# Linear attention and feed-forward on one core: another beginning, a query tile ahead, and weights cast later

## The chip, the cores and the metric

The kernel runs on one core of one Trainium2 chip. The metric is the device time of one execution in microseconds. The times shown are medians of several executions. A profiled execution is one of its own; its times are what the profile and the trace show.

## What is computed

The input `x` is 16 sequences of 1024 rows of 512 numbers. Cut to what matters, the reference is:

```python
qkv = x @ Wqkv.T + bqkv
q, k, v = split(qkv)
q, k = rope(rmsnorm(q, gq)), rope(rmsnorm(k, gk))     # 16 heads of 32
qf, kf = relu(q), relu(k)
vk = einsum('bhlp,bhld->bhpd', [v, 1], kf)             # summed over a sequence
res = einsum('bhpd,bhld->bhlp', vk, qf)
attn = res[..., :-1] / (res[..., -1:] + 1e-6)
x = layernorm(x + rmsnorm(attn @ Wout.T + bout, gout))
xr, xk = mu_r*x + (1-mu_r)*x_prev, mu_k*x + (1-mu_k)*x_prev
r = sigmoid(xr @ W_r.T);  k_act = relu(xk @ W_k.T)**2
x = layernorm(x + r * (k_act @ W_v.T))
```

## The kernel before

The rows are worked in 128 tiles of 128 rows; 8 tiles make a sequence. Every operand of a large product is held as two fp32r parts: a high part, cast by ACT (`S.copy`), and the rest, which DVE or POOL makes by subtraction. A product is then three matmuls (high by high, high by low, low by high).

The first half of the run goes through the tiles in *slots*. Slot `i`:

- loads the transposed tile `i + 2` (`load_xt`) and the plain tile `i + 1` (`load_xn`), and splits them (`split_x`, `split_xn`);
- projects tile `i` onto queries and keys (`proj(i, 0)` and `proj(i, 1)`, 12 matmuls each, L426). The bias is put into the bank ahead by a copy on ACT (`seed`, through the helper at L157); for the first two tiles it is added by two further matmuls from a row (L436);
- turns both by the rope tables (`rope`): ACT sums squares (L453), DVE multiplies twice and adds (L456 to L458), POOL takes the power (L142), ACT scales and clips the keys (L468, L469), DVE makes their low part (L470), POOL adds up the keys of the sequence (L475, L477);
- takes the rope tables of tile `i + 1` (`tables`). For the first 8 tiles they are made: one matmul (L388) and a copy by ACT (L389), one product by POOL (L385), and stores to memory (L390). Later tiles load them (L380);
- multiplies the keys of tile `i - 1` with its rows (`add_kx`, 12 matmuls, L496), summed in four banks over the sequence.

At the end of a sequence `finish_a` empties the four banks (L510 by ACT, L511 by DVE), `finish_s` sums the keys, `finish_b` and `finish_c` make the matrix that the sequence's queries are multiplied with, and `finish_c` stores it (L589, 512 KB each). They stand in slots with `i % 8` equal to 1 to 6. The 20 weight pieces that are needed later are loaded one a slot from slot 5 on (`late_weight`, the load at L352, the cast at L353, the low part at L354); 12 of them are stored again, split (L605). From slot 26 on the matrices of the first sequence are loaded (`load_m`), and from slot 30 on the first tiles of the second half are begun (`FIRST`, `STEP`).

Four banks of PSUM (`bank`) go round for projections, tables and seeds; four more (`kx_bank`) hold the key sums, and serve the beginning before that.

Ahead of slot 0 stands the beginning: ten matmuls on zeros (`NWARM`), loads of the query and key weights in eight pieces (`stage_qk`, L631, the first four turn about on the queues of SP and ACT), their split (`split_qk`, L638, L639), the bias and gain rows (L645), the masks and tables (`gt`, L705 to L707, and `cs`, L717 to L728), and the projections of tiles 0 and 1.

Order: `in_order` fixes the traced order on an engine. In the beginning it holds for all engines, for slots 0 to 7 on PE alone. Elsewhere a planner orders the instructions by its own estimate of time. `tc.issue_after` keeps loads behind a given one on SP.

The second half multiplies the queries with the matrices and does the feed-forward part (L178). Nothing there is touched.

Of the kernel before, what the change touches and what calls it, by code (L numbers as in the profile page):

```python
# [15 lines left out]
P = 128  # L16
# [8 lines left out]
NWARM = 10  # L25
# [8 lines left out]
def kernel(  # L34
# [58 lines left out]

    @contextmanager
    def in_order(engine):

        traced = nc.cur_bb.bb.instructions
        n = len(traced)
        yield
        assert traced is nc.cur_bb.bb.instructions  # L100
        last = None
        for i in traced[n:]:
            if i.engine != engine:
                continue
            if last is not None:
                tc.add_manual_dep(
                    i,
                    last.name,
                    mybir.DependencyInfo(
                        mybir.DependencyClass.NoSync, mybir.DependencyReason.DATA  # L110
                    ),
                    reason="in_order",
                )
            last = i
# [190 lines left out]
    with ExitStack() as a_ctx:  # L305
# [44 lines left out]
        def split_w(hi, lo, src, low, dma, tag="xw", bufs=3):  # L350
            w = tp.tile([P, DIM], F32, tag=tag, bufs=bufs, name="wstage")
            dma.dma_start(out=w, in_=src)  # L352
            S.copy(hi, w)  # L353
            low.tensor_sub(lo, w, f32(hi))  # L354

        first = {}

        def seed(i):
            for j in range(2):
                first[i, j] = seeded(f"ps{'qk'[j]}{i}", b_qk[:, j * DIM : (j + 1) * DIM])  # L360
# [7 lines left out]
        tab, tab_d = {}, {}  # L368

        def tables(i):  # L370

            t = i % 8
            if i < 8:
                tab_d[t] = dram.tile([P, 2, 2, DIM], F32, name=f"tab_d{t}")
            for j in range(2):
                for n in (1, 0):
                    tb = wa.tile([P, DIM], F32, tag=f"tab{j}{n}", name=f"tab{j}{n}{i}")
                    tab[i, j, n] = tb
                    if i >= 8:
                        nc.sync.dma_start(out=tb, in_=tab_d[t][:, j, n, :])  # L380
                        continue
                    g = g_qk[:, j * DIM : (j + 1) * DIM]
                    if n == 0:
                        c = angle[0][:, t, :].unsqueeze(1).to_broadcast([P, 2 * HEADS, HH])
                        G.tensor_mul(rows(tb), rows(g), c)  # L385
                    else:
                        ps = kx_bank(j) if i < 2 else bank(f"pstab{i}{j}")
                        T.matmul(ps, lhsT=cs[0:KT, t, :], rhs=gt[0:KT, j, :], start=True, stop=True)  # L388
                        S.copy(tb, ps)  # L389
                    nc.sync.dma_start(out=tab_d[t][:, j, n, :], in_=tb)  # L390
# [3 lines left out]
        def constants():  # L394
            nc.sync.dma_start(out=b_out, in_=bout.partition_broadcast(P))
            nc.sync.dma_start(out=g_out, in_=gout.partition_broadcast(P))
            for n, m in (("k", mu_k), ("r", mu_r)):
                mu[n] = const.tile([P, NC_], F32, name=f"mu_{n}")
                nc.sync.dma_start(out=mu[n], in_=m)
                omm[n] = const.tile([P, NC_], F32, name=f"omm_{n}")  # L400
                V.tensor_scalar(omm[n], mu[n], -1.0, 1.0, ALU.mult, ALU.add)
# [7 lines left out]

        mask = te.tile([P, P], BF16, name="mask")  # L410
        V.memset(mask, 0.0)
        for h in range(P // DH):
            V.memset(mask[h * DH : (h + 1) * DH, h * DH : (h + 1) * DH], 1.0)
        ones = te.tile([P, P], F32R, name="ones")
        V.memset(f32(ones), 1.0)
# [3 lines left out]
        def proj(i, j):  # L419

            seeds = i > 1
            ps = first.pop((i, j)) if seeds else bank(f"ps{'qk'[j]}{i}")
            cols = slice(j * DIM, (j + 1) * DIM)
            for c in range(NC_):
                for n, (a, b) in enumerate(((xh, "h"), (xh, "l"), (xl, "h"))):
                    T.matmul(  # L426
                        ps,
                        lhsT=a[i][:, c, :],
                        rhs=w_qk[b][:, c, cols],
                        start=(not seeds and c == 0 and n == 0),  # L430
                        stop=(seeds and c == NC_ - 1 and n == 2),
                        skip_group_check=True,
                    )
# [12 lines left out]
        acc, ros = {}, {}  # L446

        def rope(i, ps):

            ss = wa.tile([P, 2], F32, tag="ss", bufs=3, name=f"ss{i}")  # L450
            ro = []
            for j in range(2):
                S.activation(junk(f"{i}{j}"), ps[j], AF.Square, accum_out=ss[:, j : j + 1])  # L453
                r = wa.tile([P, DIM], F32, tag=f"ro{j}", bufs=1 + j, name=f"ro{j}{i}")
                t2 = wa.tile([P, DIM], F32, tag="t2", name=f"t2{j}{i}")
                V.tensor_mul(t2, ps[j], tab.pop((i, j, 1)))  # L456
                V.tensor_mul(ps[j], ps[j], tab.pop((i, j, 0)))
                V.tensor_add(halves(r), halves(ps[j]), halves(t2)[:, :, ::-1, :])  # L458
                ro.append(r)
                if j == 0:  # L460
                    q_d[i] = dram.tile([P, DIM], F32, name=f"q_d{i}")
                    nc.sync.dma_start(out=q_d[i], in_=r)
            V.tensor_scalar(ss, ss, 1.0 / DIM, RMS_EPS, ALU.mult, ALU.add)  # L463
            rsqrt(rstd_all[:, i, :], ss)
            k = ro[1]
            kh = tk.tile([P, DIM], F32R, tag="kh", bufs=2, name=f"kh{i}")
            kl = tk.tile([P, DIM], F32R, tag="kl", bufs=2, name=f"kl{i}")
            S.activation(kh, k, AF.Relu, scale=rstd_all[:, i, 1:2])  # L468
            S.activation(k, k, AF.Relu, scale=rstd_all[:, i, 1:2])  # L469
            V.tensor_sub(kl, k, f32(kh))  # L470
            b, t = divmod(i, 8)
            ros[i] = k
            if t == 1:
                acc[b] = tx.tile([P, DIM], F32, tag="acc", name=f"acc{b}")
                G.tensor_add(acc[b], ros[i - 1], k)  # L475
            if t > 1:
                G.tensor_add(acc[b], acc[b], k)  # L477
            return kh, kl
# [118 lines left out]
        def late_weight():  # L597
            n, w, c = late.pop(0)
            if n in "ao":
                to = {"a": w_a, "o": w_o}[n]  # L600
                split_w(to["h"][:, c, :], to["l"][:, c, :], w[:, c, :], V, nc.sync)
                return
            m = te.tile([P, 2, DIM], F32R, tag="m", bufs=2, name=f"w{n}{c}")
            split_w(m[:, 0, :], m[:, 1, :], w[:, c, :], V, nc.sync)
            nc.sync.dma_start(out=w_d[n][:, c, :, :], in_=f32(m))  # L605
# [7 lines left out]
        start_pe.enter_context(in_order(mybir.EngineType.PE))  # L613
        start = a_ctx.enter_context(ExitStack())
        for e in ("SP", "Activation", "DVE", "Pool"):
            start.enter_context(in_order(getattr(mybir.EngineType, e)))

        row = tp.tile([P, DIM], F32, tag="q", bufs=3, name="row")
        V.memset(row, 0.0)
        m0 = te.tile([P, 2, DIM], F32R, tag="m", bufs=2, name="m0")  # L620
        V.memset(f32(m0[:, 0, :]), 0.0)


        for n in range(NWARM):
            T.matmul(bank(f"pswarm{n}"), lhsT=m0[:, 0, 0:P], rhs=m0[:, 0, :], start=True, stop=True)
        stage = {}

        def stage_qk(j, c, dma=nc.sync):
            n = NC_ * j + c
            w = tp.tile([P, DIM], F32, name="wstage", **[dict(tag="x", bufs=NT), dict(tag="xw", bufs=3), dict(tag="q", bufs=3)][(n >= NT) + (n >= NT + 3)])  # L630
# [3 lines left out]
        def split_qk(j, c, low=V):  # L634
# [4 lines left out]
            low.tensor_sub(l, w, f32(h))  # L639
# [4 lines left out]
        for n, src in enumerate((bqkv[0 : 2 * DIM], gqk)):  # L644
            nc.scalar.dma_start(  # L645
# [3 lines left out]

        S.copy(table, mhalf)  # L650
        angle = [tp.tile([P, 8, HH], F32, tag="y", bufs=2, name=f"angle{n}") for n in range(2)]
        nc.sync.dma_start(out=angle[1], in_=sin_t)
        stage_qk(1, 0)
        load_xt(1)
        for c in range(1, NC_):
            stage_qk(1, c)
        load_xn(0)
        nc.sync.dma_start(out=angle[0], in_=cos_t)
        g_qk = wp.tile([P, 2 * DIM], F32, tag="m", bufs=NC_, name="g_qk")
        nc.sync.dma_start(out=g_qk, in_=gqk.partition_broadcast(P))  # L660
        b_qk = ca.tile([P, 2 * DIM], F32, name="b_qk")
# [20 lines left out]
        V.tensor_scalar(msk[:, 1, :], msk[:, 0, :], -1.0, None, ALU.mult)  # L682
        cs6 = wp.tile([P, 8, P], F32, tag="m", bufs=NC_, name="cs6")[:, :, 0:KT]
# [5 lines left out]
        split_qk(0, 0)  # L689
        split_qk(0, 1)  # L690
# [4 lines left out]
        split_qk(0, 2)  # L695
        split_qk(0, 3)
        ahead = {(0, 0): proj(0, 0)}
        split_x(1)
        split_qk(1, 0, G)
        split_qk(1, 1, G)  # L700
        gt = wp.tile([P, 2, DIM], F32R, tag="m", bufs=NC_, name="gt")
        for j in range(2):
# [8 lines left out]
            )  # L711
        cs = wp.tile([P, 8, P], F32R, tag="m", bufs=NC_, name="cs")
# [16 lines left out]
        split_qk(1, 2, G)  # L729
        split_qk(1, 3, G)  # L730
        ahead[1, 0] = proj(1, 0)
        tables(0)
        ahead[0, 1] = proj(0, 1)
        split_xn(0)
        ahead[1, 1] = proj(1, 1)
        start.close()

        def slot(i):
# [6 lines left out]
            qk = [ahead.pop((i, j)) if i < 2 else proj(i, j) for j in range(2)]  # L745
            if 0 < i < N - 1:
                split_x(i + 1)
            if i > 0:
                split_xn(i)
# [8 lines left out]
            if i >= 1:  # L758
                add_kx(i - 1)
            state[i] = rope(i, qk)  # L760
            if not last:
                tables(i + 1)
                if i > 0:
                    seed(i + 1)
            if i == 2:
                with tc.issue_after(load.ins):
                    constants()
            if i >= 5 and late:
                with tc.issue_after(load.ins):
                    late_weight()  # L770
            j, late_by = divmod(i - FIRST, STEP)
            if j + 1 in (0, NPRE) and late_by >= STEP - NC_:

# [321 lines left out]
```

## Time and profile before

| | us |
|---|---|
| median of the runs shown | 2727.32 (2726.01 to 2727.47) |
| the profiled execution | 2726.91 |
| its span | 2725.1 |
| PE busy in it | 2694.3 |
| DVE, ACT, POOL busy | 2168.5, 1882.8, 706.5 |
| mean granted TensorE clock | 0.997 |
| first matmul, first projection | 2.23, 7.58 |

The engines work side by side, each through its own queue in order: PE the matmuls, DVE and ACT element-wise work, POOL slow element-wise work, SP the transfers (`SPq` is its issuing, `ACTq` that of ACT). A row of the timeline gives the start, the duration, engine, line and operation, then what is written and read; the brackets give how long the engine had been idle and what ended that. The share of busy time is a mean over all stages, so it is read by stretches of time.

### The profile page before, as it was taken

The numbers are of one execution on the slowest core, as the hardware profiler recorded it, in microseconds if no ns is written. First come the engines' busy times: TensorE is split into PE (matmuls) and PEld (weight loads), VectorE is DVE, ScalarE is ACT, GpSimd is POOL, SyncE is SP. The second block draws the span as 40 slices with busy tenths as digits, with TensorE's granted clock in tenths as the row PEclk, the third lists the DMA queues.
The fourth block names the chain that finished last, engine by engine and source line by source line (L and its number), as shares of the span: only waits on it lengthen the run. The fifth ranks groups of instructions, "written<-read, shape, count | busy, mean of one in ns | idle before, by whom it ended". The sixth has DMA issues, their size and how long they took to land.

```text
span 2725.1 us, 40195 instructions
## 1 busy us (share of the span) xinstructions
PE 2694.3 (99%) x12558; PEld 2231.9 (82%) x12558; DVE 2168.5 (80%) x4876; ACT 1882.8 (69%) x3822; POOL 706.5 (26%) x804
## 2 busy tenths in 40 slices
PE   8999999999999999999999999999999999999998
PEld 6788788888888888887888888888888888888887
DVE  7878787877787787776888878888887878888874
ACT  6666565666666666657777787777777777777775
POOL 5222222222222222224322222222222222222221
PEclk9999999999999999999999999999999999999999
DMA  7689777777777877764332232323133232313210
GB/s 237 210 301 320 228 247 229 229 224 226 232 229 254 265 248 243 230 204 159 105 94 86 93 109 66 109 89 113 62 97 109 72 99 93 116 59 106 77 54 36
DMA packets 232014, 433.28 MB, mean 159 GB/s; under 512 B 24676, under 2 KB 24932, under 8 KB 231800
## 3 DMA queue, kind: packets, MB, share of 16 engines
q1 hardware_dynamic: 231504, 430.18, 49.0%
q8 instruction: 99, 1.62, 0.2%
q14 instruction: 115, 0.94, 0.1%
q10 hardware_dynamic: 296, 0.53, 0.1%
HBM read 314.19 MB, written 116.42 MB: 158 GB/s over the span
## 4 chain that ended last, share of the span: by engine, by line
PE 51%; DVE 1%; ACT 0%; issue 0%; POOL 0%; POOLq 0%; ACTq 0%
PE psk L178 12%; PE psv L178 12%; PE psr L178 12%; PE psy L178 11%; PE pst L163 2%; PE psqt L163 2%; ACT x L283 0%; DVE mixr L832 0%; DVE q L235 0%; DVE mixk L832 0%; DVE gate L973 0%; DVE mrl L848 0%; DVE qtl L247 0%; ACT gate L961 0%; DVE den L232 0%
## 5 line engine op out<-in xcount | busy, mean ns | idle before, releaser
L178 PE MATMUL psk<-mkh,w_k 128*128 128x512 f32 x1024 | 332.7, 396 | 1.1 <-DVE kx L511 0.7
L178 PE MATMUL psv<-w_v,kah 128*128 128x512 f32 x1024 | 321.6, 395 | 1.3 <-DVE gate L973 1.0
L178 PE MATMUL psy<-mb,qth 128*128 128x512 f32 x1024 | 319.9, 389 | 0.3 <-ACT qth L246 0.3
L178 PE MATMUL psr<-w_r,mrh 128*128 128x512 f32 x1024 | 318.6, 396 | 0.0
L477 POOL TENSOR_TENSOR acc<-acc,ro 128x512 f32<-128x512 f32 x96 | 159.0, 1656 | 270.4 <-ACT ro L469 227.4
L178 PEld LDWEIGHTS psy<-mb,qth 128*128 128x128 f32 x1024 | 192.0, 188 | 40.4 <-ACT qth L246 0.7
L178 PEld LDWEIGHTS psk<-mkh,w_k 128*128 128x128 f32 x1024 | 191.3, 188 | 40.3 <-DVE kx L511 1.0
L178 PEld LDWEIGHTS psv<-w_v,kah 128*128 128x128 f32 x1024 | 187.7, 188 | 38.6 <-DVE gate L973 1.5
L178 PEld LDWEIGHTS psr<-w_r,mrh 128*128 128x128 f32 x1024 | 188.7, 188 | 36.9 <-ACT r L883 0.2
L142 POOL TENSOR_TENSOR rstd_all<-ss,mhalf 128x2 f32<-128x2 f32 x128 | 93.8, 733 | 477.6 <-DVE ss L463 459.7
L848 POOL TENSOR_TENSOR mkl<-mixk,mkh 128x512 fp32r<-128x512 f32 x127 | 166.0, 1307 | 181.7 <-ACT mkh L846 177.3
L426 PE MATMUL psq<-wqk_h,xh 128*128 128x512 f32 x512 | 201.7, 394 | 4.0 <-ACT psq L157 3.2
L426 PE MATMUL psk<-wqk_h,xh 128*128 128x512 f32 x512 | 199.8, 390 | 2.5 <-ACT psk L157 2.5
L426 PE MATMUL psq<-wqk_l,xh 128*128 128x512 f32 x512 | 200.5, 392 | 0.9 <-DVE wqk_l L639 0.8
L426 PE MATMUL psq<-wqk_h,xl 128*128 128x512 f32 x512 | 200.6, 392 | 0.0
L178 PE MATMUL psv<-w_v,kal 128*128 128x512 f32 x512 | 200.1, 391 | 0.0
L178 PE MATMUL psk<-mkl,w_k 128*128 128x512 f32 x512 | 199.8, 391 | 0.2 <-DVE mkl L848 0.2
L178 PE MATMUL psy<-mb,qtl 128*128 128x512 f32 x512 | 199.6, 390 | 0.0
L426 PE MATMUL psk<-wqk_h,xl 128*128 128x512 f32 x512 | 199.3, 389 | 0.0
L426 PE MATMUL psk<-wqk_l,xh 128*128 128x512 f32 x512 | 199.3, 389 | 0.0
L178 PE MATMUL psr<-w_r,mrl 128*128 128x512 f32 x512 | 196.5, 393 | 0.0
L142 POOL TENSOR_TENSOR yrs<-yss,mhalf 128x1 f32<-128x1 f32 x128 | 70.4, 550 | 394.1 <-DVE yss L295 296.8
(189 smaller groups left out, 7165.9 us busy)
## 6 DMA issues: line engine op xcount, KB each, us to landing
tab<-tab_d SPq DMA_DIRECT2D x480, 256.0 KB, 4.3
xt<-in_xt_dram SPq DMA_DIRECT2D x128, 256.0 KB, 4.4
xn<-in_x_dram SPq DMA_DIRECT2D x128, 256.0 KB, 5.0
q_d<-ro SPq DMA_DIRECT2D x128, 256.0 KB, 3.9
m_d<-m SPq DMA_DIRECT2D x64, 512.0 KB, 5.8
mb<-m_d SPq DMA_DIRECT2D x64, 512.0 KB, 7.2
q<-q_d SPq DMA_DIRECT2D x128, 256.0 KB, 2.8
out_dram<-x SPq DMA_DIRECT2D x128, 256.0 KB, 2.2
```

Source lines behind the costliest of these rows:

```text
L142: G.tensor_tensor(dst, src, mhalf[:, 0 : src.shape[1]], ALU.pow)
L163: T.matmul(ps[:, n * P : (n + 1) * P], lhsT=b, rhs=ident, is_transpose=True, start=(n == 0), stop=(n == NC_ - 1), skip_group_check=True,)
L178: T.matmul(ps, lhsT=a[u][:, rows], rhs=b[w][:, cols], start=(afresh and c == 0 and k == 0), stop=(c == n - 1 and k == 2), skip_group_check ...
L426: T.matmul(ps, lhsT=a[i][:, c, :], rhs=w_qk[b][:, c, cols], start=(not seeds and c == 0 and n == 0), stop=(seeds and c == NC_ - 1 and n == 2),
L477: G.tensor_add(acc[b], acc[b], k)
L848: (V if by_v else G).tensor_sub(ml, m, f32(mh))
```

## The change

- The beginning: on ACT the table load and its small copy stand ahead of its loads; the gain row is loaded by SP instead of ACT, tile 1 is loaded ahead of the sine table, and the other loads change places. The first projections (`by_part=True`) take all high products first. The low parts of the key weights go from POOL to DVE, and the casts of a group stand ahead of its low parts. `NWARM` is 8. The memset for the warming matmuls comes first on DVE; masks and ones come later.
- Tiles 0 to 7 run in `early` instead of `slot`: the queries of tile `i + 1` are projected in tile `i`, behind its keys, and the keys of tile `i - 1` are multiplied after that. Tables, seeds and rope are split in a query part and a key part. Tile 2 too gets its bias by two matmuls, and its tables use two of the kx banks. From tile 3 on a table and the projection that follows share one bank. POOL's order is fixed for tiles 0 to 7.
- The constants are loaded in tile 7 instead of slot 2; two small operations on them (`omm`) stand in slot 12.
- A late weight is loaded in one slot and cast two slots later at the earliest. The loads stand in tiles 3 to 10, and then in slots 15 to 17, 31 to 33, 39 to 41 and 47 to 49.
- The matrices of the first sequence are loaded in slots 23 to 26 instead of 26 to 29, those of the second in 95 to 97 and 103 instead of 90 to 93.

```diff
-NWARM = 10
+NWARM = 8
...
+    def not_before(ins, last):
...
+    def last_of(engine):
+        return next(i for i in reversed(nc.cur_bb.bb.instructions) if i.engine == engine)
...
-        def seed(i):
-            for j in range(2):
-                first[i, j] = seeded(f"ps{'qk'[j]}{i}", b_qk[:, j * DIM : (j + 1) * DIM])
+        def seed(i, j):
+            b = b_qk[:, j * DIM : (j + 1) * DIM]
+            if (i, j) in first:
+                S.copy(first[i, j], b)
+            else:
+                first[i, j] = seeded(f"ps{'qk'[j]}{i}", b)
...
-                        ps = kx_bank(j) if i < 2 else bank(f"pstab{i}{j}")
+                    ps = kx_bank(j + 2 * (i == 2)) if i < 3 else bank(f"ps{'qk'[j]}{i}")
...
+                    if i > 2:
+                        first[i, j] = ps
...
-        def proj(i, j):
-
-            seeds = i > 1
+        def proj(i, j, by_part=False):
+
+            seeds = i > 2
...
+            three = ((xh, "h"), (xh, "l"), (xl, "h"))
+            order = [(p, c) for c in range(NC_) for p in three]
+            if by_part:
+
+                order = [(three[n], c) for n in (0, 2, 1) for c in range(NC_)]
...
-        def late_weight():
+        staged = []
+
+        def late_load(i):
             n, w, c = late.pop(0)
+            st = tp.tile([P, DIM], F32, tag="xw", bufs=3, name="wstage")
+            nc.sync.dma_start(out=st, in_=w[:, c, :])
+            staged.append((i, n, c, st))
+
+        def late_split():
+            _, n, c, st = staged.pop(0)
...
+            S.copy(h, st)
+            not_before(last_of(act), before)
+            V.tensor_sub(l, st, f32(h))
+            if n not in "ao":
+                nc.sync.dma_start(out=w_d[n][:, c, :, :], in_=f32(m))
...
+        start_pe.enter_context(in_order(mybir.EngineType.Pool))
         start = a_ctx.enter_context(ExitStack())
-        for e in ("SP", "Activation", "DVE", "Pool"):
+        for e in ("SP", "Activation", "DVE"):
...
+        m0 = te.tile([P, 2, DIM], F32R, tag="m", bufs=2, name="m0")
+        V.memset(f32(m0[:, 0, :]), 0.0)
...
+        S.copy(table, mhalf)
         stage = {}
...
-        for n, src in enumerate((bqkv[0 : 2 * DIM], gqk)):
-            nc.scalar.dma_start(
+        for n, (dma, src) in enumerate(((nc.scalar, bqkv[0 : 2 * DIM]), (nc.sync, gqk))):
+            dma.dma_start(
...
-        S.copy(table, mhalf)
+        load_xt(1)
...
-        stage_qk(1, 0)
-        load_xt(1)
-        for c in range(1, NC_):
+        for c in range(NC_):
             stage_qk(1, c)
-        load_xn(0)
...
+        load_xn(0)
...
-        split_qk(0, 0)
-        split_qk(0, 1)
+        lows = [split_qk(0, c) for c in range(NC_)]
+        for low in lows:
+            low()
...
-        ahead = {(0, 0): proj(0, 0)}
+        ahead = {(0, 0): proj(0, 0, by_part=True)}
         split_x(1)
-        split_qk(1, 0, G)
-        split_qk(1, 1, G)
+        lows = [split_qk(1, c) for c in range(2)]
...
-        tables(0)
-        ahead[0, 1] = proj(0, 1)
+        rope_table(0, 0)
+        rope_table(0, 1)
         split_xn(0)
-        ahead[1, 1] = proj(1, 1)
         start.close()
+
+        def early(i):
+
+            load = load_xt(i + 2)
+            rope(i, 0, ahead.pop((i, 0)))
+            rope_table(i + 1, 0)
+            if i > 1:
+                seed(i + 1, 0)
+            rope(i, 1, proj(i, 1, by_part=(i == 0)))
+            rope_table(i + 1, 1)
+            if i > 1:
+                seed(i + 1, 1)
+            if i > 0:
+                split_x(i + 1)
+                split_xn(i)
+                ahead[i + 1, 0] = proj(i + 1, 0)
+                add_kx(i - 1)
+            load_xn(i + 1)
+            add_keys(i)
+            late_step(i, load)
+
+        def late_step(i, load):
+            if staged and staged[0][0] <= i - 2:
+                late_split()
+            if i == 7:
+                with tc.issue_after(load.ins):
+                    constants()
...
+            if late and (3 <= i < 11 or i % 8 in (7, 0, 1) and not 23 <= i <= 26 and i > 14):
+                with tc.issue_after(load.ins):
+                    late_load(i)
+
+
+        loads_m = {23 + c: (0, c) for c in range(NC_)}
+        loads_m.update({n: (1, c) for c, n in enumerate((95, 96, 97, 103))})
...
-        for i in range(N - 1):
+        for i in range(8):
+            early(i)
+        start_pe.close()
+        for i in range(8, N - 1):
             slot(i)
-            if i == 7:
-                start_pe.close()
```

## Prediction

> **What bounds the kernel now.** First the page: span, and busy time of the matmul engine.
>
> ```profile
> span 2725.1 us, 40195 instructions
> PE 2694.3 (99%) x12558; PEld 2231.9 (82%) x12558; DVE 2168.5 (80%) x4876; ACT 1882.8 (69%) x3822; POOL 706.5 (26%) x804
> ```
>
> PE is the bound, so the change can only pay by taking PE's waits away. To find them I read the busy time by stretch (columns: stretch, its length, then busy time of PE, PEld, DVE, ACT, POOL, the granted PE clock, DMA share, GB/s):
>
> ```profile
> 0.00:24.00 24.00, 20.16 (x80) 15.43 (x81) 15.75 (x29) 12.65 (x25) 12.56 (x24) 1.00 0.73 243
> 24.00:36.00 12.00, 8.73 (x30) 6.27 (x28) 9.21 (x17) 6.33 (x13) 6.21 (x5) 0.86 0.83 269
> 36.00:50.00 14.00, 13.97 (x61) 11.55 (x62) 9.89 (x15) 10.12 (x21) 8.36 (x6) 1.00 0.59 208
> 50.00:84.00 34.00, 31.34 (x133) 24.32 (x133) 27.65 (x39) 23.12 (x47) 17.74 (x15) 1.00 0.67 224
> 84.00:110.00 26.00, 23.69 (x98) 19.12 (x97) 20.95 (x33) 16.14 (x36) 4.82 (x4) 0.93 0.65 213
> 110.00:250.00 140.00, 138.01 (x639) 114.66 (x638) 111.22 (x197) 86.32 (x182) 34.73 (x29) 1.00 0.87 292
> 250.00:310.00 60.00, 56.13 (x251) 45.05 (x250) 46.61 (x84) 33.67 (x74) 12.10 (x11) 0.97 0.81 265
> 310.00:1200.00 890.00, 889.67 (x4127) 743.38 (x4126) 709.93 (x1313) 548.71 (x1158) 210.95 (x196) 1.00 0.75 237
> ```
>
> From 310 to 1200 PE is never idle; the waits lie before 310, and that is all the changed code (the slots). Busy time understates them: a matmul of 512 columns is drawn 390 ns long, but its successor starts 227 ns later when nothing holds it (median over each of the large matmul groups). So I count as lost what a start-to-start exceeds 227 ns by (113 or less for the short ones). Lost: 1.66 us in 7.5–24, 4.47 in 24–31.9, 1.09 in 31.9–36.2, 0.06 in 36.2–50, 4.08 in 50–84, 4.20 in 84–110, 2.80 in 110–250, 7.18 in 250–310, 1.64 in 310–1200, 8.74 in 1200–1350. Before 7.58, where the first projection starts, nothing useful runs. Then the timeline of PE, for who ends these waits:
>
> ```profile
> 27.35 2.13 PE L496 MATMUL pskx<-kh,xnh 128*128 128x512 f32 x4 [2.50 <-ACT tab L389]
> 60.84 0.50 PE L426 MATMUL psq<-wqk_h,xh 128*128 128x512 f32 x1 [0.89 <-ACT psq L157]
> 105.41 0.50 PE L426 MATMUL psq<-wqk_h,xh 128*128 128x512 f32 x1 [2.31 <-ACT psq L157]
> 181.14 0.96 PE L496 MATMUL pskx<-kh,xnh 128*128 128x512 f32 x3 [1.63 <-DVE kx L511]
> 300.30 1.91 PE L496 MATMUL pskx<-kl,xnh 128*128 128x512 f32 x4 [1.88 <-DVE kl L470]
> ```
>
> And the timeline of ACT, for what ACT itself waited for just before:
>
> ```profile
> 4.48 0.49 ACTq L645 DMA_DIRECT2D row<-in_gqk_dram  x1
> 5.00 1.28 ACT L650 ACT_TABLE_LOAD   x1 [5.00 <-DMA xt<-in_xt_dram]
> 6.39 0.61 ACT L327 CAST xh<-xt 128x512 fp32r<-128x512 f32 x1
> ...
> 103.63 0.62 ACT L353 CAST wout_h<-wstage 128x512 fp32r<-128x512 f32 x1 [3.45 <-DMA wstage<-in_wout_dram]
> ...
> 294.57 0.62 ACT L342 CAST xnh<-xn 128x512 fp32r<-128x512 f32 x1 [5.24 <-DMA xn<-in_x_dram]
> ```
>
> ACT works in order. At 103.63 it stands 3.45 us before the cast of a weight whose load was issued only at 100.50; the seed of the next projection is queued behind, and PE's 2.31 us at 105.41 are that wait passed on. The same shape, smaller, stands at 56.26 (1.04), 74.84 (1.15) and 95.69 (2.50).
>
> **A rule weighed: what an idle stretch of PE costs.** After the waits at 27.35, 105.41 and 300.30 matmuls start 427 ns apart for 3.4 us each (granted clock 0.86, 0.93, 0.97 in the rows above); after the 1.63 us at 181.14 they don't. So each of the three cost 1.6 us more than its idle time. The Trainium skill ("TensorE: Matmul & The Clock Gate", section "HAM oscillation — how this bites in real kernels") gives the rule as no idle gaps over some 3.4 us; by it gaps of 2 us lose no clock and removing these three pays 4.8 us less. The row decides: idle of 1.9 to 2.5 us did halve the clock. My losses above hold both.
>
> **The change, part by part.**
>
> *The beginning.* ACT's table load (1.28 us) moves from 5.00 to the front, about 0.8 to 2.2 with its copy. It then no longer stands between tile 0's landing (at 4.48 at the latest, when the issue behind it was let go) and cast xh, which can start near 4.5 instead of 6.39. But the table load now stands ahead of ACT's own issues: wstage 1 and 3 go out at 2.25 and 2.7 instead of 0.73 and 1.18. Before they had landed by 5.93 and 6.88 (when the loads that wait for them were issued); plus 1.5 that is 7.4 and 8.4 at worst, unchanged at best since less is in front. Middle: the fourth high cast ends at 7.9. The low parts no longer come between (order by part): four high products by 8.0, four with xl (0.91) by 8.9, lows by DVE at 0.6 each behind the casts, two bias rows (0.45): psq0 is done near 10.2 against 12.38. Four psb products (0.93), eight transposes (0.8), 14 products of psq1 (3.2): the tables of tile 0 start at 15.1 against 17.36. DVE takes the low parts of the key weights from POOL: four at 0.6 instead of POOL's 1.3 to 1.7; in its order xl1, gt, two lows, cs end near 14.9, just in time. On SP, row<-gqk is the seventh and xt1 the eighth load; eight are out before the first has to wait for a landing in the trace, so sin becomes the ninth and leaves near 4.5, its copy cs is needed only at 11. Gain 2.3.
>
> Against it: NWARM 8 gives 8 x 427 ns = 3.4 us of warming, and PE then waits for casts. The trace has the step to 227 ns only after ten warm products (2.23 to 6.67). The Trainium skill (same page, "Part 1: The HAM clock gate") says that the clock is released after about 3.4 us of sustained work in a window that runs freely; 3.4 us fill such a window only by luck. If it comes one window later, some 6 products more run at half speed: 1.2 us; if not, 0. Two load queues alone bring nothing: both were used before, and the skill ("DMA: Bandwidth & Descriptors", "Issuing engines are not separate DMA queues") allows only issue time. I take 2.0 for the beginning, bounds 0.3 and 3.3.
>
> *A new wait.* rope_table(1,0) now stands on PE right behind tile 0's tables and writes the same bank. Before, the copy of that bank started 0.43 us after its product and took 0.55: PE waits about 0.55, and behind it proj(0,1). Minus 0.55.
>
> *q a tile ahead, tiles 0 to 7.* Between the end of psk0 and add_kx(0) PE now has three table products (0.7) and two projections of 14 (6.4), 7.1 us, where it had 3.7. The chain from psk0 to kh is three DVE operations (1.9), ss (0.15), POOL's power (0.7), kh (0.7): 3.5 us, and up to 3 us of other DVE work (xl2, rope of q1). It fits by half a microsecond: of the 4.47 lost in 24–31.9 I leave 0.3. Tile 2 gets its bias by rows: 4 products, 0.91 on the path; two seeds of 0.59 leave ACT.
>
> *Tiles 3 to 10.* The seed now goes into the bank that the table just left, so a tile takes two banks of the four instead of four, and a bank is free a tile earlier. A weight's cast comes two slots, some 17 us, behind its load instead of 3 to 5. That is what ended the waits at 36.03, 60.84, 64.69, 83.29 and 105.41, 9.43 us from 31.9 to 110. Constants move from slot 2 to 7, where SP issues two more loads of 256 KB and three small ones; SP's next waits there are loads needed a slot later. What is late next is DVE: in 50–84 it does 27.65 us of work against 29.9 of PE's, 92%. I leave 2.0. POOL's order is fixed for tiles 0 to 7: the key sum stands ahead of the next tile's table, which by the sums above is wanted 4 us later; hidden, at up to 1.8 (one acc) a tile if not.
>
> *From slot 8.* In 110–250 the largest wait is 1.79 at 181, where ACT had stood 1.21 for a weight's load; half goes. In 250–310 four loads of mb (512 KB) met four stores of m_d (512 KB) in slots 26 to 29, and xn came 5.24 us late; the loads move to 23 to 26, where no m_d is stored and now no weight is loaded. Of 9.98 I leave 2.6. In return nine weights are loaded in slots 31 to 49, cast by ACT (0.55) and DVE (0.65) with DVE 80% busy: hidden, or a wait like that at 181 (1.63) at three sequence ends, 4.9. I take 1.0. Gain 6.4.
>
> Sum: 2.0 - 0.55 + 4.17 - 0.91 + 7.43 + 6.4 = 18.5 us. The profiled execution took 2726.91 (span 2725.1), so 2708.4; the median of the runs shown is 0.41 above it: 2708.8, I say 2709.
>
> **The rivals.**
> - *DVE becomes the bound in slots 2 to 10* (92% already, with POOL's work beside it stretching xl from 0.68 to 1.3): 5 us more stay, 2714. For it: DVE's share; against it: DVE's idle there is mostly its waiting for weights (3.01 at 56.91, 3.86 at 96.35).
> - *Only the beginning pays.* From slot 8 ACT's and DVE's order is the planner's, and another load jams where these did; the gain is 4.7, 2722.6. Against it: each wait above has its own named load.
> - *Slower: the start of each sequence.* At 181 the first product of a new sequence waits for DVE to clear the kx bank. The sequences after it start without a wait, because of an order that the planner chose for code that now differs. If the new order asks for the bank as early as at 181 in all 14 sequences from there on, each pays 1.8: 25 us, 2734. It decides from (18.5 + 5.5)/14 = 1.7 us each. For it: the row at 181.14; against it: 889.67 of 890 busy with a slot that hardly changes.
>
> **How the numbers follow.** This kernel's measurement can tell 0.2%, 5.5 us, from no change. The forecast has 0.63 (2702 to 2716: all bounds good gives 25, all bad 11), DVE 0.18, only the beginning 0.11, slower 0.08. The range 2702 to 2721 leaves out the slower case, most of the third and a tail. Faster 0.82, same 0.10, slower 0.08.
>
> **What would show it.** First projection near 6, tile 0's tables near 15; no wait over 0.6 before the first pskx; granted clock 1.00 from 24 to 36 and from 84 to 310; no cast of a weight with a DMA ahead of it; mean PE wait under 3 us in 32–110. It is wrong if pskx still waits over 1 us at the starts of sequences, if wqk_h's fourth cast ends past 9, or if ACT stands over 2 us for any load.

## The result, and the profile after

The changed kernel takes 2708.5 us (median of 6 runs, 2706.84 to 2709.84) against 2727.03 for the kernel before (6 runs, 2724.66 to 2727.47). The ratio is 0.9934, with a 95% interval of 0.9921 to 0.9946: 18 us, 0.66%. The profiled execution took 2708.87, with a span of 2707.1.

The page of the changed kernel, its span and its busy times:

```profile
span 2707.1 us, 40178 instructions
PE 2688.8 (99%) x12560; PEld 2230.7 (82%) x12560; DVE 2175.3 (80%) x4880; ACT 1883.2 (70%) x3820; POOL 695.6 (26%) x800
```

Its busy time by stretch, the same stretches and columns as before:

```profile
0.00:24.00 24.00, 21.31 (x84) 16.09 (x85) 19.89 (x37) 14.86 (x30) 8.75 (x22) 1.00 0.83 280
24.00:36.00 12.00, 9.75 (x36) 7.59 (x35) 11.10 (x15) 6.93 (x14) 7.63 (x6) 0.86 0.78 268
36.00:50.00 14.00, 14.00 (x63) 11.54 (x62) 9.86 (x16) 9.45 (x20) 6.39 (x6) 1.00 0.71 235
50.00:84.00 34.00, 33.81 (x149) 27.57 (x148) 28.39 (x42) 24.20 (x49) 17.18 (x14) 1.00 0.72 226
84.00:110.00 26.00, 26.00 (x132) 22.16 (x131) 24.16 (x41) 17.09 (x36) 4.83 (x5) 1.00 0.79 255
110.00:250.00 140.00, 140.00 (x635) 116.47 (x634) 117.18 (x200) 88.59 (x187) 32.52 (x30) 1.00 0.82 268
250.00:310.00 60.00, 60.00 (x284) 50.28 (x283) 47.48 (x87) 35.48 (x76) 15.54 (x14) 1.00 0.81 256
310.00:1200.00 890.00, 889.35 (x4124) 741.76 (x4123) 711.99 (x1314) 550.63 (x1160) 211.00 (x196) 1.00 0.76 243
```

From 36 us on PE hardly stands any more, and the granted clock is 1.00 from 36 to 310. One stretch did not get well: 24 to 36 has PE at 9.75 of 12 us and the clock at 0.86, as before. The timeline of PE shows the waits that are left in the beginning:

```profile
5.59 1.02 PE L429 MATMUL psq<-wqk_h,xh 128*128 128x512 f32 x2 [0.34 <-ACT wqk_h L667]
7.03 1.02 PE L429 MATMUL psq<-wqk_h,xh 128*128 128x512 f32 x2 [0.41 <-ACT wqk_h L667]
...
16.22 0.51 PE L391 MATMUL psb<-gt,cs 96*128 96x512 f32 x1 [0.44 <-ACT tab L392]
...
26.87 0.84 PE L505 MATMUL pskx<-kh,xnh 128*128 128x512 f32 x3
29.96 0.79 PE L505 MATMUL pskx<-kh,xnh 128*128 128x512 f32 x1 [2.25 <-ACT tab L392]
30.55 1.91 PE L505 MATMUL pskx<-kh,xnl 128*128 128x512 f32 x4
```

Three products of add_kx(0) run at 26.87 as forecast, the keys being ready. The fourth waits 2.25 us, and not for keys: it is ended by ACT's copy of a rope table. After it matmuls start 427 ns apart for 3.4 us (the row at 30.55 is the beginning of that). The timeline of ACT at that place gives the cause one step further back:

```profile
25.33 0.73 ACT L475 ACTIVATE ro<-ro,rstd_all 128x512 f32<-128x512 f32 x1
26.16 0.59 ACT L392 COPY tab<-psb 128x512 f32<-128x512 f32 x1
29.32 0.59 ACT L392 COPY tab<-psb 128x512 f32<-128x512 f32 x1 [2.57 <-DVE t L461]
```

Tile 2's tables lie in the third and fourth kx bank, where add_kx(0) begins its sum. The copy out of the fourth bank writes the tile that holds tile 1's table, and so waits until DVE has used that one (L461). The edit also orders ACT's squares of tile 2's queries behind this copy (`before_q2` in the kernel), which the list of changes leaves out.

To compare the two traces in spite of their different orders I add up what matmul starts lose over 227 ns (half or less for short ones) between marks that both have: the first projection, tile 0's tables, and the first product of `add_kx` of tiles 0, 1, 8 and 32.

| stretch | before, lost us | after, lost us |
|---|---|---|
| start to the first projection | 7.58 | 5.59 |
| to tile 0's tables | 1.61 | 1.39 |
| to add_kx(0) | 2.72 | 0.82 |
| to add_kx(1) | 2.91 | 4.18 |
| to add_kx(8) | 8.32 | 0.63 |
| to add_kx(32) | 12.62 | 2.85 |
| to the last matmul | 23.91 | 25.09 |

Some 0.95 per sequence in these sums is not lost: products of odd sizes stand at its end. So 2.85 over three sequences is nothing. The table adds up: 19.1 us less, and 0.9 for the four bias products more, make the 18.2 by which the last matmul starts earlier (2717.36 and 2699.16).

### The profile page after: what moved, and what is told of

Read it like the earlier page. It is cut to its first block, busy times and chain, and to the rows that moved or that the text cites. A ratio compares the mean times of both kernels' runs of the same rounds, so it can differ in the third digit from the quotient of the medians.

```text
span 2707.1 us, 40178 instructions
## 1 busy us (share of the span) xinstructions
PE 2688.8 (99%) x12560; PEld 2230.7 (82%) x12560; DVE 2175.3 (80%) x4880; ACT 1883.2 (70%) x3820; POOL 695.6 (26%) x800
## 4 chain that ended last, share of the span: by engine, by line
PE 51%; DVE 1%; ACT 0%; issue 0%; POOL 0%; POOLq 0%; ACTq 0%
PE psk L183 12%; PE psv L183 12%; PE psr L183 12%; PE psy L183 11%; PE pst L168 2%; PE psqt L168 2%; ACT x L288 0%; DVE mixr L901 0%; DVE q L240 0%; DVE mixk L901 0%; DVE gate L1042 0%; DVE mrl L917 0%; DVE qtl L252 0%; ACT gate L1030 0%; DVE den L237 0%
```

## Experiments: what the casts are worth

Each kernel was timed beside the kernel before, in three groups on three chips (its medians there: 2728.87, 2726.31 and 2726.67). Across groups the ratios are the safer comparison. Each kernel left one trace, of one execution. Line numbers move by a few between kernels.

**Casts at once in the changed kernel.** The cast stands in the slot of its load; the order that holds it behind ACT's last operation traced before it stays.

```diff
-            if staged and staged[0][0] <= i - 2:
-                late_split()
...
                     late_load(i)
+                late_split()
```

> The changed kernel, but each late weight is cast in the slot of its load, loads in the same slots as in the changed kernel. Theory (ACT stands before the cast until the load lands, and seeds are queued behind): waits of 1 to 3.5 us of ACT for weights come back in tiles 3 to 10, and 5 to 8 us of the 9.4 lost there before, so about 2714 to 2717. Rival (shared banks and the query a tile ahead gave enough slack to swallow ACT's waits): within 2 us of the changed kernel, about 2709.

Measured: 2705.62 (2704.8 to 2709.41), ratio 0.992 (0.9906 to 0.9934). The rival held: nothing came back. In the trace the casts start 10.8 to 19.7 us behind the issue of their loads (in the changed kernel 22 to 40, in the kernel before 3.1 to 6.1 for the first six), and ACT waits for no weight. The time is even 2.9 us below the changed kernel's. The traces put that elsewhere than in tiles 3 to 10: 1.50 us are lost instead of 4.18 at add_kx(0) and 1.9 fewer behind add_kx(32), with tile 0's tables 1.35 later. So the lag of two slots is not needed. Either slack swallowed the waits, as the rival said, or the order alone keeps the casts late. The next two runs tell these apart.

**The same without the order.**

```diff
-            act = mybir.EngineType.Activation
-            before = last_of(act)
             S.copy(h, st)
-            not_before(last_of(act), before)
```

> The changed kernel, each weight cast in the slot of its load, and without the order that holds the cast behind ACT's last operation traced before it. With that order the casts came 11 to 20 us behind their loads and ACT waited for no weight. Theory (it is the place of the cast in ACT's order that counts, however it is brought about): without it the planner puts casts 3 to 6 us behind their loads as in the kernel before, ACT waits 1 to 4 us at some of the weights in tiles 3 to 10, and 3 to 8 us come back: 2709 to 2714. Rival (the planner with the query a tile ahead places them late by itself): about 2705.6, as with the order.

Measured: 2722.74 (20 runs, 2718.17 to 2725.9), ratio 0.9982 (0.9976 to 0.9989); 17 us came back, more than the theory's 8. By the two traces 9.3 of them lie between add_kx(2) and add_kx(8). Another 2.9 lie at add_kx(0), where the wait is for a bank and not for a cast, and the rest later; the beginning was 1.5 faster. The casts start 3.5 to 5.7 us behind the loads in tiles 3 to 10. The timelines of ACT and then PE in this run show the chain whole:

```profile
50.04 0.72 ACT L474 ACTIVATE kh<-ro,rstd_all 128x512 fp32r<-128x512 f32 x1
54.51 0.62 ACT L623 CAST wa_h<-wstage 128x512 fp32r<-128x512 f32 x1 [3.76 <-DMA wstage<-in_wqkv_dram]
55.04 0.72 ACT L475 ACTIVATE ro<-ro,rstd_all 128x512 f32<-128x512 f32 x1
55.66 0.60 ACT L347 CAST xnh<-xn 128x512 fp32r<-128x512 f32 x1
56.17 0.57 ACT L392 COPY tab<-psq 128x512 f32<-128x512 f32 x1
56.77 0.59 ACT L360 COPY psq<-b_qk 128x512 f32<-128x512 f32 x1
```

```profile
57.42 0.50 PE L429 MATMUL psq<-wqk_h,xh 128*128 128x512 f32 x1 [2.45 <-ACT psq L360]
```

ACT stands 3.76 us before the cast, then works off what is queued behind it, and only the fourth operation behind the cast, the seed, lets PE go. Such waits halved the clock twice between 36 and 110 (at 58.0 and 85.3, 3.4 us each). Between add_kx(2) and add_kx(8) 9.63 us are lost, against 0.34 with the order: the query ahead and the shared banks gave no slack for waits of this size.

**Order, and order with lag, in the kernel before.** The order alone:

```diff
+            act = mybir.EngineType.Activation
+            before = next(k for k in reversed(nc.cur_bb.bb.instructions) if k.engine == act)
             S.copy(hi, w)
+            cast = next(k for k in reversed(nc.cur_bb.bb.instructions) if k.engine == act)
+            tc.add_manual_dep(cast, before.name, ..., reason="in_order")
```

> The kernel before, and only an order that holds each late weight's cast behind ACT's last operation traced before it; slots, loads and lag as before. Theory: the first six casts, 3.1 to 6.1 us behind their loads before, come over 10 us behind; ACT's waits for weights of 1.0, 1.2, 2.5 and 3.5 us go, and the time is near that of the two-slot lag alone, 2718 to 2721. Rival (the lag of two slots is needed): 2725 to 2727.

Measured: 2718.7 (2716.36 to 2722.91), ratio 0.9973 (0.9962 to 0.9984). The theory held. The casts come 11 to 24 us behind their loads, and of 8.27 us lost between add_kx(2) and add_kx(8) 1.58 are left (in the trace of its slowest execution).

The lag (`late_load` and `late_split` two slots apart, from slot 4 on), which has the order too:

```diff
-            if i >= 5 and late:
+            if staged and staged[0][0] <= i - 2:
+                late_split()
+            if i >= 4 and late:
                 with tc.issue_after(load.ins):
-                    late_weight()
+                    late_load(i)
```

> The kernel before, and only the late weights' casts two slots behind their loads; the loads start one slot earlier (slot 4), one a slot as before. Theory: ACT's waits for weights go; of 9.4 us lost in 32 to 110, the 5 us behind the waits at 56, 75, 95 and 103 go (the clock's 1.7 among them) and some 1.2 us at 179: about 2721. The wait at 27.35 stays. Rival (seeds wait for free banks, not for ACT): the waits stay, 2726 to 2727.

Measured: 2718.62 (2715.51 to 2719.69), ratio 0.9964 (0.995 to 0.9977), 1.29 lost where 8.27 were. The two gained 7.6 and 10.2 us in their groups, and their ratios' intervals overlap. What they share is that the cast stands late in ACT's order. A lag without the order was not run.

## Experiments: beginning, query ahead and slots

**Beginning and query ahead without the rest.** As the unordered kernel above, with one weight a slot from slot 5, constants in slot 2 and the matrices' loads where they were.

```diff
-            if i == 7:
+            if i == 2:
                 with tc.issue_after(load.ins):
                     constants()
...
-            if late and (3 <= i < 11 or i % 8 in (7, 0, 1) and not 23 <= i <= 26 and i > 14):
+            if late and i >= 5:
...
-        loads_m = {23 + c: (0, c) for c in range(NC_)}
-        loads_m.update({n: (1, c) for c, n in enumerate((95, 96, 97, 103))})
+        loads_m = {26 + c: (0, c) for c in range(NC_)}
+        loads_m.update({90 + c: (1, c) for c in range(NC_)})
```

> The changed kernel's beginning and tiles 0 to 7 with the query ahead, and all else as before: late weights one a slot from slot 5, cast at once and without order, matrices loaded in slots 26 to 29 and 90 to 93, constants in slot 2. Theory (beginning and query ahead pay some 2 and 4 us less 1.5 of new costs, and slack from shared banks takes part of the seeds' waits): 2716 to 2720. Rival (the shared banks take nearly all of them): 2709 to 2712. Rival (without the lag nothing of tiles 3 to 10 is gained): 2722 to 2724.

Measured: 2728.25 (21 runs, 2724.18 to 2732.7), ratio 1.0007 (1.0001 to 1.0014). All three expectations missed: these parts alone gain nothing. Tile 0's tables are 2.2 us earlier, but between add_kx(0) and add_kx(1) 6.92 us are lost (2.91 before), since here the wait for the kx bank is 4.5 us long, as the timeline of PE shows:

```profile
32.19 0.80 PE L505 MATMUL pskx<-kh,xnh 128*128 128x512 f32 x1 [4.50 <-ACT tab L392]
```

Constants load beside it; whether that lengthens it was not tried. The waits for weights stay (8.14 between add_kx(2) and add_kx(8)). The trace is of the slowest of the 21 executions, 2732.7. The beginning and the query ahead were not run apart.

**Tile 2's copied tables in tiles of their own.**

```diff
-                tb = wa.tile([P, DIM], F32, tag=f"tab{j}{n}", name=f"tab{j}{n}{i}")
+                if i == 2 and n == 1:
+                    tb = tp.tile([P, DIM], F32, tag="x", bufs=NT, name=f"tab{j}{n}{i}")
+                else:
+                    tb = wa.tile([P, DIM], F32, tag=f"tab{j}{n}", name=f"tab{j}{n}{i}")
```

> The changed kernel, and tile 2's two copied rope tables go into tiles of their own, so that their copies out of the kx banks need not wait for DVE's use of tile 1's tables. Theory: the one large wait left, before the fourth matmul of add_kx(0) (2634 ns from start to start at 27.33, 2.4 us lost, and 3.4 us at half clock behind it, 1.7 us), comes from those copies (ACT's copy at 29.32 waited 2.57 us for DVE); it goes, and the span falls by about 4.1 us, from 2707.1 to about 2703. Rival: the keys' low part (kl of tile 0, done at 28.64) or a bank would hold the same products a moment later, and less than 1.5 us is gained.

Measured: 2705.29 (2703.87 to 2707.6), ratio 0.9917 (0.9904 to 0.9931); span 2702.8. Between add_kx(0) and add_kx(1) 0.07 us are lost instead of 4.18, and the clock is not halved there. The cause is shown; the kernel with twelve warming matmuls (below) has the same edit, starts tile 0's tables at 15.11 as the changed kernel does, and loses 0.05 there. The two kernels were timed in different groups and their intervals overlap; by the traces the gain at this place is 4.1, of which the beginning of that run took 1.3 back (below).

**The matrices' loads in their old slots, in the changed kernel.**

```diff
-        loads_m = {23 + c: (0, c) for c in range(NC_)}
-        loads_m.update({n: (1, c) for c, n in enumerate((95, 96, 97, 103))})
+        loads_m = {26 + c: (0, c) for c in range(NC_)}
+        loads_m.update({90 + c: (1, c) for c in range(NC_)})
```

> The changed kernel, but the matrices of the first and second sequence are loaded in slots 26 to 29 and 90 to 93 again. Theory (these loads of 512 KB collide with the stores of finish_c in slots 27 to 30): most of the 7.2 us lost in 250 to 310 comes back, about 2713 to 2716, with ACT waiting some 5 us for xn near slot 30. Rival (with no weights' loads in slots 18 to 30 the queue has room): within 1.5 us of the changed kernel.

Measured: 2709.77 (2708.87 to 2711.65), ratio 0.9934 (0.9921 to 0.9947). The rival held for the first sequence: between add_kx(24) and add_kx(32) 0.96 us are lost, as in the changed kernel. In this one trace the second sequence's loads do cost, 6.52 between add_kx(64) and add_kx(96) against 3.9 to 4.0; by time the two kernels are not to be told apart.

**The same move alone, in the kernel before.**

```diff
-            if j + 1 in (0, NPRE) and late_by >= STEP - NC_:
+            if i in loads_m:
                 with tc.issue_after(load.ins):
-                    load_m((j + 1) // 8, late_by - (STEP - NC_))
+                    load_m(*loads_m[i])
```

> The kernel before, and only the loads of the matrices moved to slots 23 to 26 and 95 to 97 and 103. Theory: the 7.2 us lost in 250 to 310 fall to 2 or less: 2720 to 2722. Rival (in slots 23 and 24 they now meet late weights' loads and stores, the last of which are there): the wait for xn moves there and 4 us or more stay: 2723 to 2727.

Measured: 2722.27 (21 runs, 2719.97 to 2725.45), ratio 0.9984 (0.9978 to 0.9991). The theory held: from add_kx(24) to add_kx(32) 2.10 are lost instead of 7.59. In the kernel before the move is worth some 4 us; in the changed one that stretch no longer needs it. Either it or the new slots of the weights takes that jam away.

**The weights' slots.** Slots 4 to 23 in the changed kernel, lag and order kept.

```diff
-            if late and (3 <= i < 11 or i % 8 in (7, 0, 1) and not 23 <= i <= 26 and i > 14):
+            if late and i >= 4:
```

> The changed kernel, but its late weights are loaded one a slot in slots 4 to 23 as in the kernel before, casts two slots behind and held in ACT's order. Theory (the place of the cast is what matters, the slots little, save that stores of 512 KB now fall in slots where sequences end and in slot 23 and 24 on loads of the matrices): 1 to 3 us lost, 2709 to 2711. Rival (spreading the loads is what emptied 110 to 310): 5 us or more come back there, 2713 to 2716.

Measured: 2714.38 (2711.72 to 2717.61), ratio 0.9952 (0.9938 to 0.9965). The rival held: 12.44 us are lost from add_kx(8) to add_kx(32) against 2.85. At 180.08 ACT stands 3.00 us for xn:

```profile
180.08 0.62 ACT L347 CAST xnh<-xn 128x512 fp32r<-128x512 f32 x1 [3.00 <-DMA xn<-in_x_dram]
```

So the slots are worth some 5 to 6 us of their own by the ratios and medians. The trace, of the slowest execution, has more.

**The table load behind ACT's loads again.**

```diff
-        S.copy(table, mhalf)
         stage = {}
...
-        for n, (dma, src) in enumerate(((nc.scalar, bqkv[0 : 2 * DIM]), (nc.sync, gqk))):
+        for n, (dma, src) in enumerate(((nc.scalar, bqkv[0 : 2 * DIM]), (nc.scalar, gqk))):
...
+        S.copy(table, mhalf)
         load_xt(1)
```

> The changed kernel, but the table load and its copy stand behind ACT's loads again, and the gain row is loaded by ACT. Theory: the row's issue waits for a landing, the table load starts near 5, cast xh near 6.3 instead of 3.7, the first projection near 7.5 instead of 5.6; but the high casts that follow have their loads landed, so the tables of tile 0 start near 17 instead of 15.2 to 16.5: 1 to 2 us lost, about 2710. Rival (the table load first holds back ACT's two weights as much as it gains): no change, 2708.5.

Measured: 2708.93 (2707.46 to 2710.46), ratio 0.9934 (0.9921 to 0.9946): not to be told from the changed kernel's time. In its trace cast xh starts at 6.11 and the first projection at 7.29, as the theory said, and tile 0's tables start at 18.24. That it doesn't show in the time is partly that this run lost 1.50 instead of 4.18 at add_kx(0). So most of what the beginning gains is lost again at the bank: tile 0's tables start 3.1 us apart in the two traces, add_kx(1) only 0.5 (40.13 and 40.64). What the table load's place is worth stays open; it is of the size of the scatter.

**Both faster edits together, and twelve warming matmuls.** First the tables apart and the casts at once:

> The changed kernel with both edits that were faster than it: tile 2's copied tables in tiles of their own, and casts in the slot of the load, held behind ACT's last operation. Theory (the wait in add_kx(0) is one cause, the casts are another): the 1.5 us that stayed between the starts of add_kx(0) and add_kx(1) with the casts at once fall to 0.1, so about 2704, span 2702. Rival (both took away the same wait, the rest is the moment at which the clock is released): 2705 to 2706, no better than either.

Measured: 2706.24 (2705.1 to 2708.46), ratio 0.9925 (0.9913 to 0.9937). The wait is gone (0.07), but the time is no better than with either edit; the rival held. Then the same with

```diff
-NWARM = 8
+NWARM = 12
```

> The kernel b1 with twelve warming matmuls instead of eight. They then end near 6.6 instead of 4.9, where the second high cast is ready. Theory (the clock is released at the end of a stretch of 3.4 us of work whose place varies from run to run; with eight it came at 6.0 once and near 10.4 three times): the release comes near 10.4 less often, by 9.4 at most; up to 1.3 us are gained in such runs, the first projection is 1 us later but the tables of tile 0 at most 0.3: 2703 to 2704. Rival (waiting in line behind warming matmuls costs as much): as b1 or up to 1 us slower.

Measured: 2705.45 (2704.08 to 2708.39), ratio 0.9922 (0.9909 to 0.9936). Its span, 2702.3, is the shortest of all profiles, with tile 0's tables at 15.11; by time it is not to be told from the other three near 2705.5. So four versions lie 2 to 3 us below the changed kernel by their medians. The interval of each ratio overlaps its interval, and which of them is best is below what was measured.

## Why the prediction was right, point by point

The total was forecast at 18.5 us and came at 18.5. That hides two errors that cancelled, 3.0 us too much for the query ahead and 3.4 too little from slot 8 on: that the sum is so close is luck.

- *The beginning, 2.0 forecast: 2.2.* The first projection starts at 5.59 (near 6), tile 0's tables at 15.15 (15.1). Terms on the way were wrong: the cast of xh starts at 3.69 (near 4.5), the fourth high cast ends at 7.50 (7.9), and ACT's loads do not go out 1.5 us later. They are issued at 0.90, while the table load runs from 0.72 to 2.00, as the timeline of ACT shows:

```profile
0.72 1.28 ACT L652 ACT_TABLE_LOAD   x1 [0.72 <-PEq L1147]
0.90 0.87 ACTq L659 DMA_DIRECT2D wstage<-in_wqkv_dram  x2
1.99 1.07 ACTq L674 DMA_DIRECT2D row<-in_bqkv_dram  x1
```

- *The clock after eight warming matmuls, 0 to 1.2 forecast: both ends were seen.* In the changed kernel's trace the granted clock goes to full at 6.04. In three experiments that leave the beginning alone (tables apart, casts at once, matrices' loads late) it did so at 10.43, 10.34 and 10.57, and tile 0's tables start at 16.47 to 16.64, 1.3 to 1.5 us later. The Trainium skill ("TensorE: Matmul & The Clock Gate", What's actually happening) says that the window in which activity is watched runs freely, so that the step shifts by some 0.5 us from run to run. That it shifts, these traces show; by 4.4 us here, far more than the page has for sustained work. Here PE stands between the eight warming matmuls and the casts.
- *The new wait for tile 0's table copy, 0.55: 0.61* (838 ns from start to start; the row at 16.22 shows 0.44 of it as idle).
- *The query a tile ahead, 4.17 less 0.91 forecast: this step failed.* The keys' chain fits, as worked out: kh is cast at 24.58, before it is asked for. But the step took add_kx(0)'s operands for all that it needs, and left out its bank. The prediction's own row at 27.35 names ACT's copy of a table, not the keys, as what ended that wait in the kernel before. 4.18 us are lost there, 2.4 of waiting and 1.7 of halved clock. Together with the wait for the table copy and the bias products the part cost 0.3 where a gain of 2.7 was forecast; the run with tile 2's tables apart gets 4.1 back.
- *Tiles 3 to 10, 7.4 forecast: 7.7 from add_kx(1) to add_kx(8).* The mechanism was named rightly, ACT standing before a cast; that the lag of two slots does it was not: the order alone does. One wait was put to the wrong cause: the one at 36.03 comes before the first late weight is even loaded, at 51.30, and order with lag keeps it (1.78 us idle at 38.42). DVE did not become the bound: it has 28.39 of 34 us in 50 to 84 with PE at 33.81.
- *From slot 8, 6.4 forecast: 9.8.* The terms left over were too large: 2.6 for old waits and 1.0 for new ones are both nothing to be seen. The wait at 181 is gone whole, and the weights in slots 31 to 49 cost nothing that the trace shows.
- Behind add_kx(32) 1.2 us more are lost, which nothing was forecast for. They lie between 918 and 1067, where most of the other traces lose nothing. No experiment was aimed at it.
- *The rivals.* The sequences after the first start without a wait (140.00 of 140 and 889.35 of 890), so the slower case is out. "Only the beginning pays" is out too: 7.7 and 9.8 of the 18.2 us lie behind add_kx(1).
- *The signs it named.* Three failed. The granted clock from 24 to 36 is 0.86 instead of 1.00. The first sequence's pskx waits 2.25 us, where over 1 us was to mean that it is wrong. ACT stands 2.0 to 2.2 us for xn three times between 644 and 871, which cost PE nothing to be seen.
- *The rule on idle stretches of PE* (same page, HAM oscillation: none over about 3.4 us). An idle stretch of 2.25 us, at 29.96, again halved the clock for 3.4 us, so a shorter one than the page names can do it. But the prediction's row is no rule by length either: other traces have idle of 2.5 us at full clock. What fits all of them is in the last section.

## What to carry to other kernels

An operation that waits for a transfer holds up all that stands behind it on its engine. Look for the wait on PE, go back to the engine that ended it, and ask what that engine stood before; then move the waiting operation later in the order, by any means. When an operation is moved ahead, list its output bank and who still has to empty it, not only its operands. And judge a part where its own wait stands: beginning and query ahead together gained nothing in the kernel before, with 4.5 us of waiting for the bank, while with tile 2's tables apart the trace puts the query ahead at some 3.8 us by the count above.

## What the runs showed of the hardware that was not expected

- A table load on ACT does not hold up the transfers that ACT issues: they start at 0.90 beside a table load from 0.72 to 2.00, and at 0.73 where the table load comes later.
- The length of an idle stretch of PE does not alone decide whether the clock halves. In the kernel before 2.50 us of idle ahead of add_kx(0) halved it (the row at 27.35, clock 0.86 from 24 to 36). With order and lag the same wait was as long, and the clock stayed full, as the timeline of PE and then the busy time by stretch of that run show:

```profile
29.68 1.45 PE L496 MATMUL pskx<-kh,xnh 128*128 128x512 f32 x4 [2.51 <-ACT tab L389]
```

```profile
24.00:36.00 12.00, 9.31 (x38) 6.81 (x38) 11.10 (x20) 6.13 (x14) 6.44 (x6) 1.00 0.81 258
```

- What fits all fourteen traces is a grid. In the records of the granted clock all changes of one trace lie whole multiples of 3.413 us apart, to 0.03 us. Cut each trace into such steps and add up PE's idle time in each as the profile has it, leaving out the first 13 us and the end. The clock halved behind each of the 13 steps with 1.82 to 3.27 us of idle that began at full clock, and one with 2.34 kept it halved; it halved behind none with 1.78 or less. The 2.50 us before 27.35 lie in one step, the 2.51 before 29.68 in two (1.22 and 1.29). So one and the same wait can cost its length or 1.7 us more, as it falls.
- With the same eight warming matmuls the step to full speed came at 4.4 to 6.8 us or at 10.3 to 11.0; twice, having come at 4.55 and 4.39, it was followed by a halved clock again from 7.8 to 8.0, for 3.4 us. With twelve it came at 4.87, in the one profile taken.
